# A state space layer on one core: table bursts moved to even steps, half of dt x B beside them, layer norm stretched, the mask's rows written later

## The chip, the core and the metric

The kernel runs on one core of a Trainium2 chip. A core has a matrix engine (TensorE, "PE" in the profile), three engines for elementwise work (VectorE "DVE", ScalarE "ACT", GpSimd "POOL"), and a queue engine (SyncE, "SP") from which this kernel issues all its transfers. The engines run side by side; each works through its own instructions in order and waits on semaphores where it needs another's result. The metric is the device time of one execution in microseconds (us). Lower is better.

## The reference

Two layers act on x of shape (4, 384, 64, 64). Both are added to their input, and both first normalise it over 32 groups of channels.

The first layer is a state space model over the 4096 positions of each image. Cut to what matters here:

```python
xn = layernorm(groupnorm(x)) over the 384 channels
xb, z = in_proj(xn)                    # 2 x 768 channels
xc = silu(causal_conv4(xb) + conv_b)
dt_r, B, C = x_proj(xc)                # 24 + 16 + 16
dt = softplus(dt_w @ dt_r + dt_b)      # 768 channels
h[t] = exp(dt[t] * A) * h[t-1] + (dt[t] * xc[t]) * B[t]     # 16 states a channel
y[t] = sum over states of h[t] * C[t] + D * xc[t]
out = out_proj(y * silu(z))
```

The second layer is attention in a window of 7 x 7 around each pixel, 12 heads, with a bias `rel_bias` for each head and place in the window.

## The kernel before

**Chunks and steps.** The first layer takes the 4 images one after the other, each in 11 chunks of 372 or 376 positions (44 chunks). A chunk has `STEPS` = 24 steps: 6 blocks of 128 channels (d) times 4 groups of 4 states (g). One step, in the loop over s (lines 752 to 829), does for group s:

- ScalarE: four decays exp(dt * A) (`decay`, into 3 buffers in PSUM called da);
- VectorE: four scans along the positions (`scan`, one for each state), which leave h;
- GpSimd: the multiply of the group before, h(s-1) by C, in place, and one half of a dt x B product for a later group;
- TensorE: the sums of h(s-2) over the states, by transposing matmuls into one accumulator (`sums`).

**dt x B.** The input of a scan, "db", is dt * xc times B for four states. Groups of even number get theirs from VectorE, of odd number from GpSimd, each in two halves of two states (`drive`). VectorE reads dt * xc from PSUM (dtxps), GpSimd from a copy (dtx). VectorE makes the first half for group s+2 in step s and the second half in step s+1, each between its first and its second scan (line 773).

**The state.** The last column of each scan is copied away by ScalarE (line 778), since GpSimd then overwrites h. The copy for group s-1 is placed in step s, after two decays of group s. GpSimd's multiply waits for it.

**Work of other chunks.** All that prepares a chunk (load, group norm `gn`, layer norm `ln_mean`, `ln_by`, `ln_square`, `ln_var`, `ln_rstd`, then `in_proj`, `conv`, `x_proj`, `dt_mm`, loads of weights and of rows of B and C) and all that finishes it (`gate`, `out_proj`, `residual`, statistics of the output) is spread by hand over the steps of the chunks before and after. `put(o, kind, fn)` (lines 555 to 607) puts a function o steps after the chunk's first step into a list of that step; `run(s, kind)` carries it out at a fixed place of the step: one task of ScalarE between decay 2 and decay 3 (or the dtx copy there, in every third step of four), the others after the scans, then the burst, then TensorE's tasks, VectorE's, the statistics ("STAT"), and at the end SP's. The class `Written` keeps each engine's instructions in that order. Matmul results go to one of 3 PSUM banks (`bank`), handed out in turn.

**Bursts.** The decays need the table of exp; silu and softplus need other tables. So for each chunk there are three bursts on ScalarE (`silu` of xc, `softplus`, `silu` of z; lines 447 to 504): a table load, six activations, a table load back. They stand at steps 14, 19 and 3 of a chunk (offsets -10, -5 and 3). In `softplus`, two dt matmuls are made ahead, and each activation frees a bank for the next one.

**Statistics of an image.** While an image runs, the next image's x is loaded and its group statistics taken (`batch_stats`); `stats_steps` (lines 178 to 225) then spreads them over channels in five pieces, on TensorE, VectorE and ScalarE.

**The mask.** The attention needs its bias as a table in DRAM (bm) that is filled with a large negative number and then written in rows of seven by 96 transfers (lines 160 to 174), ahead of everything else of the first layer on SP's queue. The attention layer reads it at its start (line 1117).

Of the kernel before, what the change touches and what calls it, by code (L numbers as in the profile page):

```python
# [30 lines left out]
TM = max(SIZES)  # L31
TB = 3
STEPS = ND * NQ
TX = 512
NXT = L // TX
GROUPS = 32
# [46 lines left out]
def two_layers(  # L83
# [77 lines left out]
    with tc.tile_pool(name="fill", bufs=1) as fpool:  # L161
        fill = fpool.tile([QB, NH * NK], F32, name="fill")
        nc.gpsimd.memset(fill, MASKED)
        nc.sync.dma_start(bm, fill)
    with nc.allow_non_contiguous_dma(reason="rows of seven, once"):
        for qi in range(RB):
            for h in range(NH):
                dst = bass.AP(
                    bm.tensor,
                    bm.offset + qi * (CB * NH * NK + CW) + h * NK,  # L170
                    [[NH * NK + 1, CB], [CW, WS], [1, WS]],
                )
                src = rel_bias[h].unsqueeze(0).broadcast_to([CB, WS, WS])
                nc.sync.dma_start(dst, src)

    x1s = [dram.tile([C, L], F32, tag="x1", name=f"x1_{b}", bufs=NB) for b in range(NB)]

# [49 lines left out]
    def state_space_layer(eng):  # L227
# [5 lines left out]
        with ExitStack() as es:  # L233
# [49 lines left out]
            def tile_of(shape, tag, bufs, home=sb):  # L283

                if tag not in free:
                    free[tag] = [
                        home.tile(shape, F32, name=f"{tag}{k}") for k in range(bufs)
                    ]
                    for t in free[tag]:
                        kind_of[id(t)] = tag  # L290
                return free[tag].pop(0)
# [17 lines left out]
            def at(step, fn, *args):  # L309
                todo.setdefault(step, []).append((fn, args))  # L310
# [174 lines left out]
            def dt_mm(X, d):  # L485
                T = chunks[X][3]
                made[X]["dtp", d] = ps = bank()
                te.matmul(
                    ps[:, :T], w_dt[:, d * P : (d + 1) * P], made[X]["xd"][:DTR, :T],
                    start=True, stop=True,  # L490
                )
                if d == ND - 1:
                    done(made[X].pop("xd"))

            def softplus(X):
                T = chunks[X][3]
                for d in range(ND):
                    t = made[X]["dt", d] = tile_of([P, TM], "dt", 7)
                    ps = made[X].pop(("dtp", d))
                    se.activation(t[:, :T], ps[:, :T], AF.Softplus, bias=dtb[:, d : d + 1])  # L500
                    done(ps)
                    if d + 2 < ND:
                        dt_mm(X, d + 2)
                exp_tables()


# [49 lines left out]
            for X, (b, i, t0, T) in enumerate(chunks):  # L556
                S = STEPS * X

                def put(o, kind, fn, *args, S=S, X=X):
                    at((S + o, kind), fn, X, *args)  # L560

                put(-44, SP, load_x)
                for j in range(NJ):
                    put(-40 + j, ACT, gn, j)
                put(-36, PE, ln_mean)
                put(-34, DVE, ln_by, "mu", ALU.subtract)
                put(-33, ACT, ln_square, 0)
                put(-33, ACT, ln_square, 1)
                put(-32, PE, ln_var, 0)
                put(-32, PE, ln_var, 1)  # L570
                put(-32, ACT, ln_square, 2)
                put(-31, PE, ln_var, 2)
                put(-30, ACT, ln_rstd)
                put(-29, DVE, ln_by, "rs", ALU.mult)
                put(-29, ACT, halo)
                for d, o in enumerate((-26, -25, -24, -22, -20, -18)):
                    put(o - 3, SP, load_w, d)
                    put(o, PE, in_proj, d)
                    put(o + 1, ACT, in_bias, d)
                for d, o in enumerate((-23, -21, -19, -17, -15, -13)):  # L580
                    put(o, PE, conv, d)
                    put(o + 1, ACT, conv_bias, d)
                put(-10, BURST, silu, "xc")
                put(-9, PE, x_proj, 0)
                put(-8, PE, x_proj, 1)
                put(-7, ACT, x_rows)
                for k, o in enumerate((-11, -10, -9, -7, -4, -4)):
                    put(o - 3, SP, load_w, ND + k)
                    put(o, PE, in_proj, ND + k)
                    put(o + 1, ACT, in_bias, ND + k)  # L590
                for d in range(2):
                    put(-6, PE, dt_mm, d)
                put(-5, BURST, softplus)
                for o, which, g in (
                    (-4, "B", 0), (-3, "B", 1), (-2, "B", 2), (-2, "C", 0),
                    (-1, "B", 3), (-1, "C", 1), (0, "C", 2), (1, "C", 3),
                ):
                    put(o, SP, load_bc, which, g)
                put(3, BURST, silu, "z")
                for d in range(ND):  # L600
                    put(4 * d + 8, DVE, gate, d)
                for o, m, half in ((29, 0, 0), (30, 0, 1), (32, 1, 0), (33, 1, 1), (36, 2, 0), (36, 2, 1)):
                    put(o, PE, out_proj, m, half)
                for m, load_at, o, so in ((0, 28, 31, 38), (1, 31, 34, 38), (2, 35, 38, 43)):
                    put(load_at, SP, load_res, m)
                    put(o, DVE, residual, m)
                    put(so, DVE, out_stats, m)

            def batch_stats(b):
                S = STEPS * NCHUNK * b  # L610
                pieces = [(j, k) for k in range(NCHUNK) for j in range(NJ)]
                for n, (j, k) in enumerate(pieces):
                    o = S - STEPS * NCHUNK + STEPS * (n // 4) + (3, 3, 19, 19)[n % 4]
                    cell = []

                    def begin(j=j, k=k, cell=cell):
                        cell.append(x_stats(b, j, k))

                    def use(cell=cell):
                        cell.pop()()  # L620

                    at((o - 3, SP), begin)
                    at((o, DVE), use)
                cell = []

                def start():
                    cell.append(x_norm(b))

                at((S - 51, DVE), start)
                for k in range(5):  # L630
                    at((S - 50 + k, "STAT"), lambda: next(cell[0]))

            for b in range(1, NB):
                batch_stats(b)
            for b in range(NB):
                cell = []

                def begin(b=b, cell=cell):
                    cell.append(
                        stats_steps((te, ve, se.activation, done), mv1[b], gm1[b], bank, f"b{b}")  # L640
                    )

                S = STEPS * (NCHUNK * (b + 1) - 1)
                at((S + 44, "STAT"), begin)
                for k in range(5):
                    at((S + 44 + k, "STAT"), lambda cell=cell: next(cell[0]))


            cell = []
# [15 lines left out]
            def run(step, kind, only=None):  # L665
                tasks = todo.get((step, kind), [])
                part = tasks if only is None else tasks[:only]
                if only is not None:
                    todo[step, kind] = tasks[only:]
                else:  # L670
                    todo.pop((step, kind), None)
                for fn, args in part:
                    fn(*args)
# [4 lines left out]
            def drive(engine, r, half):  # L678
                X, d, T = block(r)
                g = groups[r][2]  # L680
                if half == 0:
                    drives[r] = tile_of([P, NG, TM], "db", 3)
                src = dtxps if engine is ve else dtx[X, d]
                sl = slice(2 * half, 2 * half + 2)
                engine.tensor_tensor(
                    drives[r][:, sl, :T], src[:, :T].unsqueeze(1).broadcast_to([P, 2, T]),
                    made[X]["B", g][:, sl, :T], ALU.mult,
                )
                if half == 1 and d == ND - 1:
                    done(made[X].pop(("B", g)))  # L690
                if half == 1 and g == NQ - 1:
                    done(dtx.pop((X, d)))
# [56 lines left out]
                    )  # L749
                done(yt)  # L750

            for s in range(-44, N + 28):
                r = s if 0 <= s < N else None
                g = s % NQ

# [13 lines left out]

                half = s % 2  # L770
                q = s + 2 - half
                if 0 <= q < N:
                    drive(ve, q, half)
                if 0 <= s - 1 < N:
                    X, d, T = block(s - 1)
# [38 lines left out]
                if g == 1 and (k := at_block(-3)):  # L814
                    X, d, T = k
                    se.copy(dtxps[:, :T], made[X]["dt", d][:, :T])
                run(s, DVE)
                run(s, "STAT")
                q = s + 1 + half
# [356 lines left out]
```

## Time and profile before

| what | value |
|---|---|
| median of 3 runs (lowest to highest) | 7939.66 us (7924.37 to 7944.17) |
| the profiled execution, its own time | 7920.43 us |
| its span in the profile | 7918.7 us |
| busy: PE, DVE, ACT, POOL | 6700.7, 6161.5, 5183.3, 6065.7 us |
| start until GpSimd's first dt x B (prologue) | 222.2 us |
| from there to the end of the last multiply by C | 5628 us |
| the attention layer after it | 2068 us |

Lines in the profile name an engine, an operation and the tiles as out<-in. Nearly all instructions have the line L66, that of the helper that keeps the order, so they are told apart by tiles: "h<-da,state,db" is a scan, "da" a decay, "db" a half of dt x B, "h<-h,BC" the multiply by C, "state<-h" the copy of the state, "dt<-mm" a softplus, "xc<-xc" and "sz<-sz" the silus, "mm<-mm" the two activations of `ln_rstd`. What stands after a vertical bar or in square brackets is idle time of the engine just before, and what ended it. SPq is the time in which SP issues a transfer.

### The profile page before, as it was taken

Reading aid. Unit: us, or ns where it says so; the run is one execution under the profiler, and the core shown is the slowest. Engines: PE = TensorE matmul, PEld = TensorE weight load, DVE = VectorE, ACT = ScalarE, POOL = GpSimd, SP = SyncE. Lnnn points to the kernel's source line nnn. Section 1 sums busy time; section 2 is a strip of 40 time slices with the busy share of each in tenths; the row PEclk is TensorE's granted clock in tenths of the full one; section 3 lists DMA queues with packets and bytes.
Section 4 is the critical chain, followed back from the end, with each engine's and each line's share of the span. In section 5 each row is a group of like instructions: output and inputs, shape, how many; then the busy total and the mean of one; then the engine's idle time right before and its main releaser. Section 6 shows DMA issues by size and latency. Waiting matters only on the chain.

```text
span 7918.7 us, 133479 instructions
## 1 busy us (share of the span) xinstructions
PE 6700.7 (85%) x46968; PEld 4369.9 (55%) x46968; DVE 6161.5 (78%) x10561; ACT 5183.3 (65%) x12246; POOL 6065.7 (77%) x3015
## 2 busy tenths in 40 slices
PE   3888888888888888888888888888879899899998
PEld 2555555555555555555555655555545455455555
DVE  1799999999999999999998999999955444444444
ACT  1777777777777767777777777777735455455555
POOL 0899999999999999999998999999964333333333
PEclk9899999999999999999999999999889999999999
DMA  2323323132323222232322222222223222222332
GB/s 83 97 75 97 94 76 100 62 101 69 99 74 96 84 76 89 82 95 73 104 67 92 64 92 68 90 84 77 86 59 96 91 90 91 90 91 90 96 95 80
DMA packets 467012, 677.10 MB, mean 86 GB/s; under 512 B 48317, under 2 KB 424397, under 8 KB 466149
## 3 DMA queue, kind: packets, MB, share of 16 engines
q1 hardware_dynamic: 466340, 668.56, 27.3%
q8 instruction: 371, 6.08, 0.3%
q14 instruction: 301, 2.46, 0.1%
HBM read 582.92 MB, written 85.65 MB: 84 GB/s over the span
## 4 chain that ended last, share of the span: by engine, by line
DVE 29%; PE 28%; ACT 16%; issue 10%; POOL 9%; DMA 5%; SPq 3%; DVEq 0%; POOLq 0%; ACTq 0%
DVE h L66 20%; PE mm L66 17%; POOL h L66 6%; DVE db L66 5%; ACT da L66 5%; ACT L66 4%; PE pt L66 3%; POOL db L66 3%; PE yps L66 3%; DMA o<-x 3%; SPq L66 2%; PE lg L66 2%; PE ov L66 2%; ACT sz L66 2%; ACT xc L66 2%
## 5 line engine op out<-in xcount | busy, mean ns | idle before, releaser
L66 DVE TENSOR_TENSOR_SCAN h<-da,state,db 128x372 f32<-128x372 f32 (+1 forms) x3840 | 3581.6, 983 | 384.5 <-ACT da L66 288.3
L66 POOL TENSOR_TENSOR h<-h,BC 128x1488 f32<-128x1488 f32 (+1 forms) x1056 | 3541.4, 3354 | 291.9 <-ACT state L66 291.5
L66 ACT ACTIVATE da<-dt,nega 128x372 f32<-128x372 f32 (+1 forms) x4224 | 2378.9, 572 | 614.4 <-DVE h L66 597.0
L66 PE MATMUL yps<-ident,h 128*124 128x128 f32 (+1 forms) x12672 | 1764.6, 294 | 555.1 <-POOL h L66 536.3
L66 PEld LDWEIGHTS yps<-ident,h 128*124 128x124 f32 (+1 forms) x12672 | 1558.9, 150 | 903.1 <-POOL h L66 808.3
L66 POOL TENSOR_TENSOR db<-dtx,BC 128x744 f32<-128x744 f32 (+1 forms) x1056 | 1882.9, 1783 | 59.2 <-DMA BC<-bcrows 47.6
L66 POOL TENSOR_TENSOR sg<-sg,rs 128x784 f32<-128x784 f32 x384 | 573.2, 1493 | 1025.9 <-DVE rs L66 895.4
L66 ACT ACTIVATE sg<-sg,mx 128x196 f32<-128x196 f32 x1536 | 684.8, 447 | 779.0 <-DVE mx L66 777.9
L66 PE MATMUL mm<-xn,w_in 128*128 128x372 f32 (+3 forms) x3168 | 1148.9, 503 | 9.7 <-ACT sz L66 5.8
L66 DVE TENSOR_TENSOR db<-dtxps,BC 128x744 f32<-128x744 f32 (+1 forms) x1056 | 966.6, 915 | 1.2 <-DMA BC<-bcrows 0.6
L66 PEld LDWEIGHTS mm<-xn,w_in 128*128 128x128 f32 x3168 | 610.2, 205 | 361.6 <-issue 60.8
L66 PE MATMUL mm<-xb,dcv 128*128 128x372 f32 (+1 forms) x2112 | 719.8, 484 | 0.0
L66 DVE CUSTOM_DVE_ANT_0 sg<-lg,bias 128x196 f32<-128x196 f32 x1536 | 462.6, 357 | 298.1 <-PE lg L66 297.8
L66 PE MATMUL mm<-xp,w_qkv 128*128 128x512 f32 x1092 | 539.1, 632 | 116.7 <-DVE o L66 116.2
L66 PE MATMUL mm<-yg,w_out 128*128 128x372 f32 (+1 forms) x1584 | 540.9, 483 | 0.0
L66 PEld LDWEIGHTS mm<-xb,dcv 128*128 128x128 f32 x2112 | 397.3, 195 | 225.2 <-issue 13.3
L66 PE MATMUL pt<-ident,sg 128*98 128x128 f32 x3072 | 420.2, 279 | 4.1 <-ACT pT L66 2.3
L66 PEld LDWEIGHTS pt<-ident,sg 128*98 128x98 f32 x3072 | 319.3, 128 | 122.3 <-issue 109.4
L66 PEld LDWEIGHTS mm<-xp,w_qkv 128*128 128x128 f32 x1092 | 205.5, 202 | 323.4 <-issue 191.9
L66 PE MATMUL yps<-ident,xD 128*124 128x128 f32 (+1 forms) x792 | 152.7, 306 | 263.6 <-ACT yt L66 261.7
L66 DVE TENSOR_TENSOR_SCAN h<-da,db 128x372 f32<-128x372 f32 x384 | 334.1, 916 | 49.7 <-ACT da L66 37.2
L66 PEld LDWEIGHTS mm<-yg,w_out 128*128 128x128 f32 x1584 | 290.1, 194 | 145.2 <-issue 7.0
(111 smaller groups left out, 7149.4 us busy)
## 6 DMA issues: line engine op xcount, KB each, us to landing
BC<-bcrows SPq DMA_DIRECT2D x320, 744.0 KB
w_in<-wdr SPq DMA_DIRECT2D x528, 192.0 KB
vw<-vdr SPq DMA_DIRECT2D x512, 147.0 KB
xs<-in_x_dram SPq DMA_DIRECT2D x240, 186.0 KB
vdr<-v SPq DMA_DIRECT2D x280, 96.0 KB
xp<-x SPq DMA_DIRECT2D x32, 768.0 KB
o<-x SPq DMA_DIRECT2D x96, 256.0 KB
out_dram<-o SPq DMA_DIRECT2D x96, 256.0 KB
```

What stands on the lines that cost most here:

```text
L66: ins = made(*args, **kw)
```

## The change

- The mask's 96 transfers become tasks of SP, one at the end of each of the steps 24 to 119.
- The bursts stand at steps 14, 18 and 4 of a chunk (`BURSTS`). In these steps VectorE's second half of dt x B for group s+2 is made after the burst's scans, in the same step, and no longer in the step after.
- `softplus` has three dt matmuls made ahead, and its tiles are 8 instead of 7.
- The layer norm of a chunk begins 7 steps earlier and takes longer: load at -51 instead of -44, mean at -46 instead of -36, squares one a step from -40, `ln_rstd` at -35 instead of -30, the last multiply at -34 instead of -29.
- VectorE's work on whole tiles (the two operations of layer norm, input and output statistics) moves to the steps of the bursts.
- `x_proj`, `x_rows`, the second half of `in_proj` and the dt matmuls move by a step or two.
- The statistics of the next image begin 16 steps earlier, and their five pieces are spread over steps -66, -64, -63, -62 and -56 instead of five in a row.

```diff
+BURSTS = (4, 14, 18)
...
-    with nc.allow_non_contiguous_dma(reason="rows of seven, once"):
-        for qi in range(RB):
-            for h in range(NH):
...
-                nc.sync.dma_start(dst, src)
+    def mask_row(dq, qi, h):
+
+        dst = bass.AP(
+            bm.tensor,
+            bm.offset + qi * (CB * NH * NK + CW) + h * NK,
+            [[NH * NK + 1, CB], [CW, WS], [1, WS]],
+        )
+        with nc.allow_non_contiguous_dma(reason="rows of seven, once"):
+            dq.dma_start(dst, rel_bias[h].unsqueeze(0).broadcast_to([CB, WS, WS]))
...
-                    t = made[X]["dt", d] = tile_of([P, TM], "dt", 7)
+                    t = made[X]["dt", d] = tile_of([P, TM], "dt", 8)
...
-                    if d + 2 < ND:
-                        dt_mm(X, d + 2)
+                    if d + 3 < ND:
+                        dt_mm(X, d + 3)
...
-                put(-44, SP, load_x)
+                put(-51, SP, load_x)
                 for j in range(NJ):
-                    put(-40 + j, ACT, gn, j)
-                put(-36, PE, ln_mean)
-                put(-34, DVE, ln_by, "mu", ALU.subtract)
-                put(-33, ACT, ln_square, 0)
-                put(-33, ACT, ln_square, 1)
-                put(-32, PE, ln_var, 0)
-                put(-32, PE, ln_var, 1)
-                put(-32, ACT, ln_square, 2)
-                put(-31, PE, ln_var, 2)
-                put(-30, ACT, ln_rstd)
-                put(-29, DVE, ln_by, "rs", ALU.mult)
-                put(-29, ACT, halo)
+                    put(-50 + j, ACT, gn, j)
+                put(-46, PE, ln_mean)
+                put(-44, DVE, ln_by, "mu", ALU.subtract)
+                for j in range(NJ):
+                    put(-40 + j, ACT, ln_square, j)
+                    put(-37 + j // 2, PE, ln_var, j)
+                put(-35, ACT, ln_rstd)
+                put(-34, DVE, ln_by, "rs", ALU.mult)
+                put(-33, ACT, halo)
...
-                put(-8, PE, x_proj, 1)
-                put(-7, ACT, x_rows)
-                for k, o in enumerate((-11, -10, -9, -7, -4, -4)):
+                put(-9, PE, x_proj, 1)
+                put(-8, ACT, x_rows)
+                for k, o in enumerate((-11, -10, -8, -5, -4, -3)):
...
-                for d in range(2):
-                    put(-6, PE, dt_mm, d)
-                put(-5, BURST, softplus)
+                for d in range(3):
+                    put(-7, PE, dt_mm, d)
+                put(-6, BURST, softplus)
...
-                put(3, BURST, silu, "z")
+                put(4, BURST, silu, "z")
...
-                for m, load_at, o, so in ((0, 28, 31, 38), (1, 31, 34, 38), (2, 35, 38, 43)):
+                for m, load_at, o, so in ((0, 28, 31, 38), (1, 31, 34, 42), (2, 35, 38, 42)):
...
-                    o = S - STEPS * NCHUNK + STEPS * (n // 4) + (3, 3, 19, 19)[n % 4]
+                    o = S - STEPS * NCHUNK + STEPS * (n // 4) + (4, 4, 18, 18)[n % 4]
...
-                at((S - 51, DVE), start)
-                for k in range(5):
-                    at((S - 50 + k, "STAT"), lambda: next(cell[0]))
+                at((S - 67, DVE), start)
+                for k in (6, 8, 9, 10, 16):
+                    at((S - 72 + k, "STAT"), lambda: next(cell[0]))
...
+            for qi in range(RB):
+                for h in range(NH):
+                    at((24 + qi * NH + h, SP), mask_row, dq, qi, h)
...
-            for s in range(-44, N + 28):
+            for s in range(-51, N + 28):
...
-                if 0 <= q < N:
+                if 0 <= q < N and (half == 0 or (s - 1) % STEPS not in BURSTS):
                     drive(ve, q, half)
...
+                if s % STEPS in BURSTS and 0 <= s + 2 < N:
+                    drive(ve, s + 2, 1)
                 run(s, DVE)
```

More of the change, by code (lines that the diff above doesn't have):

```diff
@@ L164, in two_layers @@
         nc.sync.dma_start(bm, fill)
-    with nc.allow_non_contiguous_dma(reason="rows of seven, once"):
-        for qi in range(RB):
-            for h in range(NH):
[L168 to L174, printed above, removed]
+    def mask_row(dq, qi, h):
[6 more added lines that the diff above has]
+            dq.dma_start(dst, rel_bias[h].unsqueeze(0).broadcast_to([CB, WS, WS]))
     x1s = [dram.tile([C, L], F32, tag="x1", name=f"x1_{b}", bufs=NB) for b in range(NB)]
```

## The prediction

> **What bounds the kernel now.** First the page, for the busiest engine of the first layer:
>
> ```profile
> L66 POOL TENSOR_TENSOR h<-h,BC 128x1488 f32<-128x1488 f32 (+1 forms) x1056 | 3541.4, 3354 | 291.9 <-ACT state L66 291.5
> ...
> L66 POOL TENSOR_TENSOR db<-dtx,BC 128x744 f32<-128x744 f32 (+1 forms) x1056 | 1882.9, 1783 | 59.2 <-DMA BC<-bcrows 47.6
> ```
>
> One pair per step: overlapped, POOL needs 5.03 us a step (the spacing of its h rows where nothing waits), 24 steps make 120.7 us a chunk. Then the busy times of that stretch:
>
> ```profile
> 222.00:5850.00 5628.00, 4716.80 (x22620) 3250.89 (x22618) 5172.13 (x6306) 4124.93 (x8505) 5320.72 (x2130) 0.93 0.27 83
> ```
>
> POOL (fifth figure) works 5321 of 5628 us, VectorE (third) 5172. So the layer can lose at most 307 us of POOL idling. The view of waits names nearly all of it:
>
> ```profile
> POOL h L66 <- ACT state L66: 291.5, 126, 6.7
> ```
>
> The timeline of one softplus burst (the sixth of 44, in step 19 of the chunk before its own) shows the place:
>
> ```profile
> 831.41 1.28 ACT L66 ACT_TABLE_LOAD   x1
> ...
> 840.78 0.18 ACT L66 COPY state<-h 128x4 f32<-128x4 f32 x1
> 841.04 3.34 POOL L66 TENSOR_TENSOR h<-h,BC 128x1488 f32<-128x1488 f32 x1 [4.28 <-ACT state L66]
> ```
>
> POOL's multiply of group r waits for the state copy of r, which stands on ScalarE behind the burst and two decays of r+1. It had been scanned at 834.27. Call **lead** of r the time from the end of its last scan to its POOL multiply. POOL idles at burst b by (state copy − scan end) − lead. Summed over POOL's rows by place in the chunk: 42 us at step 3, 49 at 14, 171 at 19; an ordinary chunk (29 of 44) idles 5.99 us.
>
> How the lead grows: a VectorE step takes 4.37 us, or 4.82 with one more 0.45 us operation (dt multiply, gate, residual), so the lead gains 0.66 or 0.21 a step; after every burst it is 1.2.
>
> Last, the start of the kernel, in the timeline:
>
> ```profile
> 13.75 15.49 PE L66 MATMUL pb<-lnb,w_in 128*128 128x1 f32 x72 [13.75 <-DMA w_in<-in_in_wT_dram]
> 15.04 65.51 SPq L174 DMA_DIRECT2D bm<-in_rel_bias_dram  x96
> ...
> 97.60 8.14 SPq L66 DMA_DIRECT2D wdr<-w_in  x12
> ```
>
> 96 mask transfers hold SP's queue; the weights behind them come at 80.6, and ScalarE, VectorE and all that follows stand still.
>
> **What the Trainium skill says.** "ScalarE: Activation LUTs", What ACT_TABLE_LOAD costs: 1283 ns a load, and some 1380 ns of drain at a switch. The trace agrees on 1.28; the next activation follows 1.30 after the load's start, so no further drain is added here. "TensorE: Matmul & The Clock Gate", Part 1: PE falls to half rate after about one idle window of 3.4 us. The trace agrees: within softplus, one dt matmul pair takes 0.62 us in some chunks and 1.24 in others. The same page, array detail: PE's queue can only pull weight loads ahead; matmuls keep their order, which the PE rows below show too. "SBUF — State Buffer", two separate sides: VectorE with two SBUF inputs and GpSimd lock each other out for a whole instruction. At the batch statistics a 128x3 operation takes 3.25 us beside POOL, against 0.16 in the prologue.
>
> **The change, part by part.**
>
> *Mask.* The loads then wait for nothing but the fill's landing (15.0). The bias matmul ends at 29.24 and becomes the next late thing; from its copy to the first wdr issue it is 2.98 us (94.62 to 97.60), so that issue falls at 32.2, 65.4 earlier. Three gn (0.69 us each) of the third chunk and their load now stand ahead of step 0: −3. Net 62. The 96 issues return in steps 24 to 119, 0.68 us of SP each; SP issues some 31 transfers of about 0.4 us per 126 us, and what is queued behind (weights, B and C rows) is wanted two or more steps, 10 us, later. Cost 0; uncovered, 96 x 0.68 = 65 us.
>
> *Half of dt x B into the burst.* 0.83 us of VectorE leaves the step after each burst. That step is 3.65 instead of 4.48 us after its first decay, so the lead after a burst is 0.6 + 5.03 − 3.65 = 1.98 instead of 1.2.
>
> *Softplus, one matmul deeper.* From the first softplus to the end of the sixth takes 3.7 to 6.0 + 0.57 us now (offsets of the rows in all 44 chunks, mean about 5.4). With three banks filled ahead, three pairs remain: 3.4 us at full PE rate, 5.3 at half rate; I take 4.0. No xD copy (0.5) follows, since step 18 is not a third step of four.
>
> *Bursts at 4, 14, 18.* State copy after scan end: at 14 as now, 4.62 + 0.6 = 5.2. At 18 the burst starts 1.7 before the scan end (dt x B, dtx copy, last decay come first): −1.7 + 1.3 + 4.0 + 1.3 + 0.65 + 0.6 = 6.2. At 4, 3.6 (burst 5.14, no xD).
>
> *Layer norm stretched.* ln_rstd now is ScalarE's task in step 13, between decays 2 and 3, and waits for the last ln_var, which stands on PE in step 12 behind two halves of the output projection. The rows that show that queue:
>
> ```profile
> 790.48 2.67 PE L66 MATMUL mm<-xb,dcv 128*128 128x372 f32 x8
> ...
> 795.20 3.92 PE L66 MATMUL mm<-yg,w_out 128*128 128x372 f32 x12
> ...
> 798.09 0.57 ACT L66 ACTIVATE da<-dt,nega 128x372 f32<-128x372 f32 x1 [0.61 <-DVE h L66]
> ...
> 798.95 2.04 PE L66 MATMUL mm<-xn,ones_c 128*128 128x372 f32 x6
> ```
>
> Two ln_var (0.63 each, a third of the mean's 1.88) follow the convolution: the sums of step 12 start at 794.25 instead of 793.83, the last ln_var ends at 800.05, and rstd (0.96) and decay 3 end at 801.6. But decay 3 of step 13 went at 798.09. PE follows POOL (its sums wait for POOL), so this is fixed against POOL's start at 805.50: the scan ends at 802.7 and **the lead at 13 is held to 2.8**, where it would be 4.6. In the same way conv_bias(4), behind the mean on PE, holds the lead at 4 to 4.8.
>
> *The rest.* VectorE's whole-tile work (layer norm 1.25, output and input statistics 0.45 each, gate) now lies in the bursts: 3.4 us with the half of dt x B at 4, 3.0 at 14, 2.6 at 18, all inside the scan-free times of 3.0 to 4.8, 4.6 and 5.6; what does not fit would be paid one for one. x_proj, x_rows and in_proj of z move by a step or two: same counts, and PE's steps 13 to 17 hold under 4 us of work each, so PE's idle time hides them; uncovered, one in_proj is 1.9 us.
>
> The ledger of leads: 1.98 at 19, 5.4 at 4 (held to 4.8: idle 0.54), 1.98 at 5, 4.6 at 13 held to 2.8, 3.0 at 14 (idle 5.2 − 3.0 = 2.2), 1.98 at 15, plus 0.66, 0.21, 0.21 = 3.06 at 18 (idle 6.2 − 3.06 = 3.14). Sum 5.88 against 5.99: over the 29 ordinary chunks 3 us. What the bursts gain, the rstd wait takes.
>
> *Next chunk's load.* load_x at −51 needs the buffer whose last reader runs on PE in that very step, 3.4 us before POOL's multiply of step 21. 0.4 us to the issue, then about 4.3 us: the transfer of 558 KB ended 6.3 us after issue with 1.1 MB queued ahead, at a peak 390 KB/us. gn in step 22 waits some 0.7 us; hidden by the spare lead at 4.
>
> *Batch statistics.* The three boundaries now idle 11.5 us over an ordinary chunk (16.4, 19.7, 16.4). Spread out, the locked operations still cost 4.9, and 1.4 and 0.6 at the next bursts: 6.9. Gain 4.6 x 3 = 14; the second layer's statistics, with a burst at 4 instead of 3: 3 x 1.5 = 4.5. Bound: 0 to 30.
>
> Sum: 62 + 3 + 14 + 4.5 = about 84. Profiled execution 7920.4 (span 7918.7) gives 7836; the median of the runs lies 19 above the profiled time, so 7939.7 − 84 = **7856**.
>
> **Rivals.**
> 1. *The lead survives at 13* (ln_var runs earlier than I count, or PE keeps full rate). Then the lead at 14 is 4.8, idle 0.45, and with 3.4 us of softplus 2.5 at 18: 3.5 a chunk, 2.4 less, 40 x 2.4 = 96 more: 7760. For it: PE is only 84% busy; against it: step 12's own rows.
> 2. *Slower: ScalarE waits for xn in step 22.* Queue order there is fixed, so every us of gn's wait is taken from the lead. Up to 2.4 us the way to step 4 absorbs it (6.0 without wait, 3.6 needed); beyond, each costs 44 us. It takes the 84 us and a measurable loss from a wait of about 5 us, a landing 8.6 us after issue; a wait of 6: 44 x 3.6 − 84 = +74, 8015. Against it: 6.3 us was the longest landing I found, with more ahead.
> 3. *Softplus always at half PE rate*: 1.3 us more a chunk, 57 us: 7913.
> 4. *Mask issues cost as much in the loop as before it*: 62 lost, 7918.
>
> **How the numbers follow.** Forecast 0.52 (7810 to 7895), rival 1 0.24, rival 2 0.07, rivals 3 and 4 0.17. Range 7745 to 7935: it leaves out most of rival 2 and the best of rival 1. About 0.3% (24 us) is what a measurement can tell here. Faster: 0.52 + 0.24 + most of 3 and 4 (0.09) = 0.85; within 0.3%: 0.08; slower: 0.07.
>
> **What would show it.** wdr issued near 32 us and the first POOL multiply near 169 instead of 231. A new wait of ScalarE's rstd on PE of 1.5 to 2 us, 44 times; POOL idle of about 0.5, 2.2 and 3.1 us at steps 4, 14 and 18, and the chunk still near 126.5 us. The softplus activations 0.62 or 1.24 apart for the last three only. Wrong if the chunk falls to 124 us or below, or rises over 128.

## The result and the profile after

| | before | after |
|---|---|---|
| median of 4 runs (lowest to highest) | 7934.56 us (7924.37 to 7944.17) | 7829.76 us (7823.9 to 7842.14) |
| span of the profiled execution | 7918.7 us | 7822.2 us |
| start until GpSimd's first multiply by C | 231.0 us | 163.9 us |
| from there to the end of the last one | 5619.4 us | 5589.4 us |
| attention layer | 2068.3 us | 2068.9 us |

The ratio of the times is 0.987, with a 95% interval of 0.9852 to 0.9888. The three stretches of the span give -67.1, -30.0 and +0.6: together the 96.5 us by which the span is shorter.

The lines that answer to those of before follow. (The helper's line is L67 now.) First the page's group of GpSimd's multiplies:

```profile
L67 POOL TENSOR_TENSOR h<-h,BC 128x1488 f32<-128x1488 f32 (+1 forms) x1056 | 3540.4, 3353 | 263.1 <-ACT state L67 247.0
```

One multiply is as long as before (3353 ns); only the idle time ahead of them fell, from 291.9 to 263.1 us. The start of the kernel, from the timeline of SP's queue and of TensorE (start, length, operation):

```profile
15.70 0.37 SPq L146 DMA_DIRECT2D w_xp<-in_xp_wT_dram  x1
...
32.92 8.12 SPq L67 DMA_DIRECT2D wdr<-w_in  x12
...
14.41 15.49 PE L67 MATMUL pb<-lnb,w_in 128*128 128x1 f32 x72 [14.41 <-DMA w_in<-in_in_wT_dram]
```

The weights come at 15.7 instead of 80.6, the bias matmul ends at 29.90 and is what the folding of the weights now waits for, and the first wdr issue falls at 32.92 instead of 97.60.

Then the burst that the prediction showed, one step earlier in the chunk, from ScalarE's and GpSimd's timelines:

```profile
759.29 1.28 ACT L67 ACT_TABLE_LOAD   x1
760.59 2.74 ACT L67 ACTIVATE dt<-mm,dtb 128x372 f32<-128x372 f32 x5
763.81 0.57 ACT L67 ACTIVATE dt<-mm,dtb 128x372 f32<-128x372 f32 x1 [0.48 <-PE mm L67]
...
766.71 0.18 ACT L67 COPY state<-h 128x4 f32<-128x4 f32 x1
...
766.96 3.33 POOL L67 TENSOR_TENSOR h<-h,BC 128x1488 f32<-128x1488 f32 x1 [2.93 <-ACT state L67]
```

The group had been scanned at 760.96; its state is copied at 766.89. GpSimd idles 2.93 us here, where it idled 4.28.

Last, steps 11 to 13 of that chunk, from TensorE's and ScalarE's timelines:

```profile
724.16 1.41 PE L67 MATMUL mm<-sq,ones_c 128*128 128x372 f32 x4
725.41 1.47 PE L67 MATMUL yps<-ident,h 128*124 128x128 f32 x12
726.72 3.92 PE L67 MATMUL mm<-yg,w_out 128*128 128x372 f32 x12
730.48 0.79 PE L67 MATMUL mm<-sq,ones_c 128*128 128x372 f32 x2
...
731.30 0.55 ACT L67 ACTIVATE mm<-mm,eps 128x372 f32<-128x372 f32 x1 [3.20 <-PE mm L67]
```

The third variance matmul stands behind the output projection, and rstd, on ScalarE between two decays, waits 3.2 us for it. Two waits of the whole run belong to this place (total, times, longest):

```profile
ACT mm L67 <- PE mm L67: 145.0, 44, 4.2
...
DVE yg L67 <- PE mm L67: 37.1, 40, 5.6
```

The first was predicted. The second, VectorE's gate, was not; it turns out to matter below.

GpSimd's idle time by place, averaged over the 26 chunks in which no image begins or ends in either kernel (worked out from its rows, as for before): 0.16, 2.68 and 2.84 us at steps 4, 14 and 18, in all 5.7, against 6.0. At 14 it is 2.1 us in 17 of them and 3.7 or 3.8 in nine.

What parts the two kinds is TensorE's clock. The trace records the clock that TensorE was granted: at any time it is either full or half (PEclk in a view by stretches, 1.00 or 0.50). In all 17 chunks with 2.1 us it was full in the 11 us ahead of the third variance matmul; in all nine others it was half in a part of them. Two lines of TensorE's timeline show it, the sums of step 11 in the chunk above and in the eighth chunk, which has 3.7:

```profile
719.97 1.53 PE L67 MATMUL yps<-ident,h 128*124 128x128 f32 x12 [2.51 <-POOL h L67]
...
1097.46 2.82 PE L67 MATMUL yps<-ident,h 128*124 128x128 f32 x12 [2.53 <-POOL h L67]
```

The matmuls are the same, and the idle time before them nearly so. From the first multiply by C to the end of the last, the record holds 806 us at half clock before and 471 after.

The next image's statistics fall in the tenth chunk of an image before and in the ninth after. In these two chunks of three images GpSimd idles 71.1 us in all before and 54.8 after.

### The profile page after: what moved, and what is told of

Same layout as the page of the kernel before. It is cut to its first block, busy times and chain, and to the rows that moved or that the text cites. A ratio compares the mean times of both kernels' runs of the same rounds, so it can differ in the third digit from the quotient of the medians.

```text
span 7822.2 us, 133481 instructions
## 1 busy us (share of the span) xinstructions
PE 6547.3 (84%) x46968; PEld 4271.8 (55%) x46968; DVE 6160.6 (79%) x10561; ACT 5158.4 (66%) x12246; POOL 6065.6 (78%) x3015
## 5 line engine op out<-in xcount | busy, mean ns | idle before, releaser
L67 DVE TENSOR_TENSOR_SCAN h<-da,state,db 128x372 f32<-128x372 f32 (+1 forms) x3840 | 3559.7, 979 | 342.1 <-issue 202.1
L67 POOL TENSOR_TENSOR h<-h,BC 128x1488 f32<-128x1488 f32 (+1 forms) x1056 | 3540.4, 3353 | 263.1 <-ACT state L67 247.0
L67 ACT ACTIVATE da<-dt,nega 128x372 f32<-128x372 f32 (+1 forms) x4224 | 2375.6, 571 | 488.4 <-DVE h L67 464.7
L67 PE MATMUL yps<-ident,h 128*124 128x128 f32 (+1 forms) x12672 | 1711.6, 289 | 755.7 <-POOL h L67 739.8
L67 PEld LDWEIGHTS yps<-ident,h 128*124 128x124 f32 (+1 forms) x12672 | 1487.6, 146 | 1166.6 <-POOL h L67 1060.5
L67 POOL TENSOR_TENSOR db<-dtx,BC 128x744 f32<-128x744 f32 (+1 forms) x1056 | 1885.9, 1786 | 56.1 <-DMA BC<-bcrows 40.8
L67 POOL TENSOR_TENSOR sg<-sg,rs 128x784 f32<-128x784 f32 x384 | 573.2, 1493 | 1029.4 <-DVE rs L67 879.1
L67 ACT ACTIVATE sg<-sg,mx 128x196 f32<-128x196 f32 x1536 | 684.8, 447 | 780.9 <-DVE mx L67 779.8
L67 PE MATMUL mm<-xn,w_in 128*128 128x372 f32 (+3 forms) x3168 | 1123.8, 492 | 43.9 <-ACT sz L67 37.5
L67 DVE TENSOR_TENSOR db<-dtxps,BC 128x744 f32<-128x744 f32 (+1 forms) x1056 | 963.0, 912 | 3.3 <-DMA BC<-bcrows 2.7
L67 PEld LDWEIGHTS mm<-xn,w_in 128*128 128x128 f32 x3168 | 586.4, 198 | 351.7 <-ACT sz L67 47.3
L67 PE MATMUL mm<-xb,dcv 128*128 128x372 f32 (+1 forms) x2112 | 719.2, 484 | 3.2 <-DVE xs L67 2.6
L67 DVE CUSTOM_DVE_ANT_0 sg<-lg,bias 128x196 f32<-128x196 f32 x1536 | 462.4, 357 | 295.1 <-PE lg L67 294.5
L67 PE MATMUL mm<-xp,w_qkv 128*128 128x512 f32 x1092 | 536.7, 630 | 121.9 <-DVE o L67 121.7
L67 PE MATMUL mm<-yg,w_out 128*128 128x372 f32 (+1 forms) x1584 | 534.5, 479 | 0.0
L67 PEld LDWEIGHTS mm<-xb,dcv 128*128 128x128 f32 x2112 | 397.3, 195 | 228.0 <-issue 12.1
L67 PE MATMUL pt<-ident,sg 128*98 128x128 f32 x3072 | 419.6, 279 | 4.7 <-ACT pT L67 2.7
L67 PEld LDWEIGHTS pt<-ident,sg 128*98 128x98 f32 x3072 | 318.3, 128 | 123.0 <-issue 107.7
L67 PEld LDWEIGHTS mm<-xp,w_qkv 128*128 128x128 f32 x1092 | 204.0, 200 | 325.7 <-issue 189.1
L67 DVE SCALAR_TENSOR_TENSOR o<-mm,pjb,o 128x512 f32<-128x512 f32 x96 | 72.1, 751 | 376.8 <-DMA o<-x 290.1
L67 DVE TENSOR_TENSOR_SCAN h<-da,db 128x372 f32<-128x372 f32 x384 | 332.6, 914 | 45.6 <-ACT da L67 25.2
L67 PEld LDWEIGHTS mm<-yg,w_out 128*128 128x128 f32 x1584 | 286.9, 192 | 142.4 <-issue 2.7
```

What stands on the lines that cost most here:

```text
L67: ins = made(*args, **kw)
```

## The experiments

Times compare as ratios to the kernel before, run on the same chip in the same session. The theory at this point was that of the prediction: the lead that the bursts gain is lost at step 13 to rstd's wait.

**The mask alone.** The kernel before, and only the mask moved.

```diff
-                nc.sync.dma_start(dst, src)
+                    at((24 + qi * NH + h, SP), mask_row, dq, qi, h)
```

> The kernel before, with the 96 mask transfers in steps 24 to 119 and nothing else of the change. Theory (the mask is the whole gain of the start and costs nothing in the loop): 65 us less than before, about 7869 us, first weight store near 33 us, first multiply by C near 165 us, and the stretch of the first layer unchanged at 5619 us from the first multiply to the last one's end. Rival 4 (the 96 issues cost as much in the loop): no change, 7934 us, with the stretch 60 us longer.

Measured: 7862.51 us against 7926.91, ratio 0.9921 (0.9906 to 0.9936). The first multiply starts at 166.3 us instead of 231.0: 64.7 earlier, and 64.4 us is what the time fell by. The stretch from the first multiply to the end of the last is 5626.7 us, 7.3 longer than before; the four times of this kernel differ by nearly twice as much (7856.34 to 7870.01). So the 96 issues cost little or nothing where they now lie; a cost of a few us cannot be told from this.

**Half of dt x B back in the step after the burst.**

```diff
-                if 0 <= q < N and (half == 0 or (s - 1) % STEPS not in BURSTS):
+                if 0 <= q < N:
...
-                if s % STEPS in BURSTS and 0 <= s + 2 < N:
-                    drive(ve, s + 2, 1)
```

> The kernel after, with VectorE's second half of dt x B back between the scans of the step after the burst. Theory (0.83 us of lead after each burst, of which the one at 18 alone is used, since the leads at 4 and 13 are held by TensorE): idle at 18 rises from 2.8 to 3.7 us, at 14 and 4 little changes: 0.9 x 40, some 35 us more than after, 7865 us. Rival (all three bursts gain 0.83 us): 100 us more, 7930 us. Rival (the half is hidden anyway): no change.

Measured: 7947.28 us, ratio 1.0027 (1.0016 to 1.0038): 0.0157 above after, some 125 us, and slower than before although the mask's 64 us are still in it. The ledger reads like this: leads after a burst are 1.15 us instead of 1.98, as the prediction had it; the idle at 14 is 3.7 instead of 2.7, at 18 4.9 instead of 2.8. Of the 2.1 us at 18, 0.8 is the lead; most of the rest is softplus, whose sixth activation starts 4.19 us after the first on average, instead of 3.24. So only 0.8 of the 3.1 us is the price that the expectation had counted. Most of the rest came with TensorE's clock: it was half for 792 us of the first layer instead of 471, and ahead of the third variance matmul it was half in part in 25 of the 26 chunks instead of nine. The view by stretches gives its mean over the first layer as the third number from the end, for the kernel after and then for this one:

```profile
163.90:5753.33 5589.43, 4563.45 (x22600) 3152.24 (x22600) 5165.24 (x6299) 4092.69 (x8490) 5315.81 (x2128) 0.96 0.26 83
...
164.28:5871.04 5706.76, 4691.05 (x22600) 3261.71 (x22600) 5162.12 (x6299) 4111.23 (x8490) 5315.20 (x2128) 0.93 0.25 81
```

This half of dt x B is worth more than all other edits of the loop together, and those others, without it, cost time: 7947 is 84 us over what the mask alone gives. The rival was nearer, and still too low.

**Two dt matmuls ahead instead of three.**

```diff
-                    if d + 3 < ND:
-                        dt_mm(X, d + 3)
+                    if d + 2 < ND:
+                        dt_mm(X, d + 2)
...
-                for d in range(3):
+                for d in range(2):
```

> The kernel after, with two dt matmuls ahead of softplus instead of three. Theory (the softplus burst lengthens by one matmul pair, and GpSimd's idle at 18 with it, one for one): the sixth softplus begins 4.4 us after the first on the mean instead of 3.2, idle at 18 rises from 2.8 to 4.0 us: 1.2 x 40, some 48 us more than after, 7878 us. Rival (the burst's length is covered by the lead): no change.

Measured: 7830.91 us, ratio 0.9883 (0.9868 to 0.9898), which overlaps the interval of after. The sixth softplus starts 3.25 us after the first, as with three ahead. The rival's number came, but not for its reason: the edit did not take the third pair of matmuls (one dt matmul is a pair of instructions) back behind the first softplus. TensorE's timeline of a burst before (its first softplus starts at 832.71) and of one in this run (at 892.0), four pairs each:

```profile
833.33 4.03 PE L66 MATMUL mm<-xd,w_dt 24*128 24x372 f32 x8 [1.73 <-ACT dt L66]
...
891.53 3.28 PE L67 MATMUL mm<-xd,w_dt 24*128 24x372 f32 x8
```

Before, the third pair waits for the first softplus to free a bank and starts 0.62 us or more after that softplus begins, in 43 of 44 bursts. In this run it starts ahead of the first softplus in 40 of 44, and within 0.3 us of its start in the others. By the order in which the kernels hand out their three banks, the reason is layer norm: before, its variance held a bank until VectorE's last multiply, behind the burst of step 19; now that multiply stands in step 14, and the third bank is free. So what puts the third pair ahead is the free bank, with `d + 3` or with `d + 2`. Its worth shows in the bursts themselves: at full clock the sixth softplus starts 3.72 us after the first before and 2.80 after, at half clock 5.98 and 4.75. The rest of the gain is the clock: bursts near the longer of these two times were 11 of 44 before and are 3 now.

**rstd's wait taken away.** All three variance matmuls in step 11.

```diff
-                    put(-37 + j // 2, PE, ln_var, j)
+                    put(-37, PE, ln_var, j)
```

> The kernel after, with the last ln_var in step 11 beside the other two, ahead of the output projection of step 12. Theory (the wait of ln_rstd behind that projection holds the lead at 13 to 2.8 us and takes what the bursts gain): ScalarE's wait before ln_rstd falls from 3.3 us to nothing, the lead at 14 rises from 3.0 to about 4.7, GpSimd's idle at 14 falls from 2.7 us to under 0.8 a chunk, at 18 it stays at 2.8: about 80 us less than after, 7750 us. Rival (TensorE is late as a whole, and the next task that waits for it, conv_bias in step 12 or in_bias in step 14, takes the place): under 20 us less, 7810 to 7830 us.

Measured: 7822.97 us, ratio 0.987 (0.9855 to 0.9885): no change. The wait itself is gone, and yet GpSimd idles 2.9 us at 14. The view of waits names the reason:

```profile
DVE yg L67 <- PE mm L67: 74.3, 42, 7.0
...
ACT mm L67 <- PE mm L67: 4.2, 2, 2.9
```

and the timelines of VectorE and TensorE show the place:

```profile
729.43 0.55 DVE L67 TENSOR_TENSOR yg<-mm,sz 128x372 f32<-128x372 f32 x1 [1.69 <-PE mm L67]
...
727.29 1.47 PE L67 MATMUL yps<-ident,h 128*124 128x128 f32 x12
728.60 2.67 PE L67 MATMUL mm<-yg,w_out 128*128 128x372 f32 x8
```

The gate of block 1, in step 12, writes yg. There are seven yg tiles, six are in use, the seventh went to the gate of step 8: the next comes free when `out_proj` of the chunk before has read it, and its last part runs on TensorE in step 12 too. With the variance matmuls ahead of it this part starts later, and VectorE, with the scans of step 13 queued behind the gate, stands. The new theory: two waits for the same late TensorE lie side by side, and removing one only leaves the other.

**Eight yg tiles.**

```diff
-                yg = made[X]["yg", d] = tile_of([P, TM], "yg", 7)
+                yg = made[X]["yg", d] = tile_of([P, TM], "yg", 8)
```

> The kernel after, with eight yg buffers in place of seven, so that the gate of block 1 at step 12 no longer needs the buffer that the second half of out_proj, on TensorE in the same step, still reads. Theory (two waits on TensorE's step 12 hold the lead at step 13, rstd's and this gate's; in the chunks with 3.7 us of idle at step 14 the gate's ends last, in the others rstd's): the idle at 14 falls from a mean of 2.7 to 2.1 us, the others stay: 7823 - 26 = about 7800 us. Rival (rstd's wait alone sets it): idle at 14 stays at 2.7, 7830 us.

Measured: 7838.07 us, ratio 0.9885 (0.9871 to 0.99): no gain. The gate's wait is down from 40 times to 2, but the idle at 14 stays at 2.9. So in the kernel after, rstd's wait is the last to end in all chunks, also in those with 3.8 us. What makes those longer is TensorE's clock, as the two lines of step 11 above show: with the sums at 2.82 us instead of 1.53, everything behind them comes 1.3 later.

**Both waits taken away.** Eight yg tiles and the variance matmuls in step 11.

```diff
-                    put(-37 + j // 2, PE, ln_var, j)
+                    put(-37, PE, ln_var, j)
...
-                yg = made[X]["yg", d] = tile_of([P, TM], "yg", 7)
+                yg = made[X]["yg", d] = tile_of([P, TM], "yg", 8)
```

> Eight yg buffers and, besides, the three variance matmuls of layer norm all in step 11 instead of 11, 11 and 12. Theory (with the variance matmuls early, rstd's wait is gone and the gate's wait took its place; with both gone the lead at step 13 is the natural 4.6 us): VectorE's stall of 2.2 us in steps 12 and 13 goes, idle of GpSimd at 14 about 0.6 instead of 2.9 us, 44 x 2.2 = 97 us less than 7823: about 7735 us. Rival (a third task behind TensorE's late step 12 takes the place again): idle at 14 stays over 2 us, 7800 to 7830 us.

Measured: 7795.86 us, ratio 0.9833 (0.9818 to 0.9848), 0.0037 below after. Either edit alone gained nothing, both together some 30 us: the waits do stand in for each other. The idle at 14 fell from 2.7 to 1.0 us (0.6 was expected). But at 18 it rose from 2.8 to 3.8: nearly half of the expected 97 us went there. From GpSimd's timeline, step 14 and 18 of the fifth chunk:

```profile
736.99 3.34 POOL L67 TENSOR_TENSOR h<-h,BC 128x1488 f32<-128x1488 f32 x1 [0.41 <-ACT state L67]
...
761.57 3.34 POOL L67 TENSOR_TENSOR h<-h,BC 128x1488 f32<-128x1488 f32 x1 [4.46 <-ACT state L67]
```

The lead at 18 is unchanged (it starts anew at each burst); softplus is longer: its sixth activation starts 4.10 us after the first on average, and 15 of 44 bursts take over 4.5. In the burst shown it starts 4.74 us after, with the last three pairs 1.25 apart. From just before the first softplus to the sixth, TensorE's granted clock is 0.68 on average over the 44 bursts, against 0.86 in the kernel after.

**The state's copy inside the burst.** The copy of a burst step's own group goes behind the third activation instead of behind the second table load and two decays.

```diff
                     se.activation(v, v, AF.Silu)
+                    if d == 2:
+                        keep_state(now[0])
```

(and the same in `softplus`; `keep_state` holds the copy that stood in the loop, which now skips groups that have been copied.)

> The kernel after, with the copy of the state of a burst step's group placed after the third of the burst's six activations instead of behind the burst. Theory A (GpSimd's idle at 14 and 18 is the wait for this copy and nothing else): both fall by 2.0 to 2.2 us, 44 x 4 = 176 us less, 7650 us. Theory B (VectorE's chain of scans, stalled by the whole burst, is nearly as long as GpSimd's, so that what GpSimd gains at one group it waits at a later one; the most to be had is VectorE's own wait for GpSimd at step 23, 1.1 us a chunk): 0 to 47 us less, 7785 to 7830 us.

Measured: 7773.75 us, ratio 0.9803 (0.9788 to 0.9817), 0.0067 or some 53 us below after. The copy costs no further table load, as the timeline shows:

```profile
753.19 1.49 ACT L67 ACTIVATE dt<-mm,dtb 128x372 f32<-128x372 f32 x3
754.56 0.20 ACT L67 COPY state<-h 128x4 f32<-128x4 f32 x1
755.45 0.57 ACT L67 ACTIVATE dt<-mm,dtb 128x372 f32<-128x372 f32 x1 [0.68 <-PE mm L67]
```

Both kernels have 265 loads. GpSimd no longer idles at 14 and 18. It idles one group later, 1.1 us at 15 and 3.4 at 19, because the scans of that group wait for the burst's end all the same. Theory A falls, and B is right, its 47 us a little too low. VectorE's idle time at step 23, 1.06 us a chunk before the edit, is 0.03: VectorE's chain of scans, with what the bursts stall it, is now as long as GpSimd's work.

**All three.**

```diff
+                    put(-37, PE, ln_var, j)
...
+                yg = made[X]["yg", d] = tile_of([P, TM], "yg", 8)
...
+                        keep_state(now[0])
```

> Eight yg buffers, the variance matmuls early and the state's copy inside the burst, all three. Theory B: the first two take VectorE's stall of 2.2 us in steps 12 and 13 away (7735 us), the third adds only what VectorE still waits for GpSimd, up to 1 us a chunk: 7690 to 7735 us. Theory A: the third adds 2.0 to 2.2 us at step 18 and 0.6 at 14 on top: 7735 - 120 = about 7615 us.

Measured: 7726.92 us, ratio 0.9742 (0.9722 to 0.9762), 0.0128 or 100 us below after. The pair alone gained some 30 us and the copy alone 53; together it is 100, and over the pair the copy gained 69, more than the 45 that B allowed: here B's bound fails, though the time lies in its range, since the pair had been expected to gain more. Why the bound fails is not shown. What is left is the idle at 19, 3.7 us, behind softplus, which takes over 4.5 us to its sixth start in 32 of 44 chunks. TensorE's timeline of such a burst:

```profile
743.67 2.14 PE L67 MATMUL mm<-xd,w_dt 24*128 24x372 f32 x6
748.28 0.90 PE L67 MATMUL yps<-ident,xD 128*124 128x128 f32 x3 [2.46 <-ACT yt L67]
748.97 2.76 PE L67 MATMUL yps<-ident,h 128*124 128x128 f32 x12
752.63 4.08 PE L67 MATMUL mm<-xd,w_dt 24*128 24x372 f32 x6 [0.90 <-ACT dt L67]
```

The same six instructions take 2.14 us and, behind a stretch with 2.5 us of idling, 4.08. That suggested keeping TensorE busy.

**Matmuls of no use ahead of softplus**, on the kernel with both waits gone, and on the one with all three edits.

```diff
+            def warm(X, n):
+                for k in range(n):
+                    te.matmul(yps[:, TB * P : 512], ident, ident, start=True, stop=True)
...
+                put(-8, PE, warm, 4)
+                put(-7, PE, warm, 8)
```

> Eight yg buffers and early variance matmuls, as in the run of 7796 us, plus twelve matmuls of 128x128 with no use (into columns of yps that nothing reads), four in step 16 and eight in step 17, where TensorE idles before softplus. Theory (freeing the lead at 13 gained 1.9 us at step 14, but TensorE then ran softplus's matmuls at half rate in nearly every chunk, six activations in 3.7 to 4.75 us instead of 2.8 to 3.4, and gave 1 us back at 18): with TensorE kept busy the sixth softplus activation starts 2.8 us after the first, the idle at 18 falls from 3.8 to about 2.5 us, 44 x 1.3 = 57 us less: about 7740 us. Rival (the extra matmuls hold up the sums, or the rate does not depend on this idle time): 7790 to 7830 us.

> The run of 7727 us (eight yg buffers, early variance matmuls, the state's copy inside the burst) plus the same twelve matmuls of no use in steps 16 and 17. Theory: softplus there took 4.75 us in nearly every chunk; at 2.8 us the idle at 19 falls from 3.7 to about 1.8 us, 44 x 1.9 = 84 us less: about 7645 us. Rival (the scan chain has no such slack, or the rate does not depend on this idle time): 7700 to 7740 us.

In these two kernels the four matmuls of step 16 restart the sum over states that is under way in the same PSUM bank, so that part of y is lost; the instructions and their number are those intended. "PSUM — Partial Sum Buffer", rule 2 on accumulation, in the Trainium skill has the mechanism: a matmul with the start flag clears the written marks of the whole bank, whichever bytes of it are written.

Measured: 7794.3 us, ratio 0.9833 (0.9816 to 0.9849), on the first, no gain over 7795.86; and 7685.09 us, ratio 0.9694 (0.9678 to 0.971), on the second, some 40 us below the kernel without them. In both, softplus became shorter (mean start of the sixth 4.10 to 3.37, and 4.23 to 3.29 us). On the first kernel the rival's first half is right: ScalarE's copy of finished sums waits for the extra matmuls, and with it the burst (117.4 us in 85 waits, against 53.6 in 45 without the extra matmuls).

```profile
753.92 0.48 ACT L67 COPY yt<-yps 124x384 f32<-124x384 f32 x1 [1.50 <-PE yps L67]
```

On the second, the idle at 19 fell from 3.7 to 2.1 us; the expected 1.8 us in every chunk and 7645 were too good, since some bursts, most of them near an image's boundary, stay slow. The copy waits much less there, 54.1 us in 46 waits; why is not shown.

**The same matmuls where they damage nothing.** First into unread columns of dtxps, in the kernel with all three edits:

```diff
-                    te.matmul(yps[:, TB * P : 512], ident, ident, start=True, stop=True)
+                    te.matmul(dtxps[:, TB * P : 512], ident, ident, start=True, stop=True)
```

> The run of 7685 us with its twelve extra matmuls written into unread columns of dtxps, a PSUM bank in which no sum is being gathered, instead of yps. Theory (TensorE's rate alone is what they change): as before, idle at 19 about 2.1 us, 7685 us (7665 to 7705). Rival (written into a bank that ScalarE and VectorE use, they wait for those engines and hold up the sums behind them): 7720 us or more.

Measured: 7761.54 us, ratio 0.9789 (0.9773 to 0.9805), worse than without them. The rival is right:

```profile
ACT dtxps L67 <- PE dtxps L67: 154.0, 43, 5.5
```

ScalarE's copy into that bank, with the dt x B products behind it, waits for TensorE in nearly every chunk, though the columns are others. Then into yps again, but with the start flag only behind the last sum of a block:

```diff
-            def warm(X, n):
+            def warm(X, n, start):
...
-                    te.matmul(yps[:, TB * P : 512], ident, ident, start=True, stop=True)
+                    te.matmul(
+                        yps[:, TB * P : 512], ident, ident,
+                        start=start, stop=start, skip_group_check=True,
+                    )
...
-                put(-8, PE, warm, 4)
-                put(-7, PE, warm, 8)
+                put(-8, PE, warm, 4, X == 0)
+                put(-7, PE, warm, 8, True)
```

> The run of 7685 us with the same twelve matmuls into yps, but those of step 16 without the start flag and only those of step 17, behind the last sum of a block, with it, so that no sum under way is restarted. Theory (the same work on TensorE at the same places, so the same rate in softplus): idle at 19 about 2.1 us, 7685 us (7665 to 7705). Rival (the gain of that run came of the damaged sums, not of the rate): 7727 us, as without the extra matmuls.

Measured: 7688.81 us, ratio 0.9699 (0.9683 to 0.9716). As the theory has it, so the gain came of TensorE's rate and not of the damaged sums. TensorE's timeline now:

```profile
744.40 2.05 PE L67 MATMUL yps<-ident 128*128 128x128 f32 x16
747.02 0.54 PE L67 MATMUL yps<-ident,xD 128*124 128x128 f32 x3 [0.57 <-ACT yt L67]
747.40 1.47 PE L67 MATMUL yps<-ident,h 128*124 128x128 f32 x12
750.60 2.14 PE L67 MATMUL mm<-xd,w_dt 24*128 24x372 f32 x6 [1.72 <-ACT dt L67]
```

The sums take 1.47 instead of 2.76 us and the dt matmuls of softplus 2.14 instead of 4.08. This is the granted clock, as the same view shows from the first to the sixth softplus, in the burst without the extra matmuls (0.50) and then in the one with them (1.00):

```profile
752.01:756.75 4.74, 4.12 (x7) 1.93 (x8) 2.98 (x6) 2.72 (x6) 4.74 (x3) 0.50 0.00 0
...
749.98:752.78 2.80, 2.18 (x7) 1.14 (x8) 2.80 (x6) 2.69 (x7) 2.80 (x3) 1.00 0.00 0
```

GpSimd idles 2.4 us an ordinary chunk, against 5.7 in the kernel after. This is the fastest version, 3.0% under the kernel before; about 140 us of that are beyond the change under study.

## Why the prediction was right, and where not

The forecast was 7856, the time is 7830. Of the 26 us between them, 12.5 are in the sum: 84 predicted, 96.5 found between the two spans. The other 13 lie in the step from a profiled execution to the median: the profile of before is 19 us under its median of then, that of after 6. Part of the agreement is luck: the loop's idle came out near the forecast because errors of 0.3 to 0.5 us at the three bursts cancel.

- *Mask: 62 predicted, 67 found,* and 64 when done alone. The wdr issue at 32.2 was right (32.92). The 3 us for the third chunk's norm did not show. Rival 4 falls.
- *Half of dt x B: right.* The lead after each burst is 1.98 to the hundredth, and 1.15 without the move. What the prediction did not see is how much of the change hangs on it, by way of TensorE's clock.
- *Softplus: right.* Its sixth activation ends 3.8 us after the first starts, 4.0 was taken, and the two bounds, 3.4 and 5.3, are 3.37 and 5.32. Three pairs remain, as the step read. But it is the bank that layer norm no longer holds that makes room for the third, not the third call ahead, as the run with two ahead shows. Where between the bounds the bursts lie hangs on TensorE's clock, for which the prediction had no working; 4.0 was chosen between them. Rival 3, always half rate, did not happen in this kernel, but came near with all three edits (32 of 44 bursts over 4.5 us).
- *The ledger of leads: right in the chunk shown, in part by chance.* Predicted idle 0.54, 2.2 and 3.14 us at 4, 14 and 18; found there 0.2, 2.1 and 2.9, on average 0.16, 2.7 and 2.8. The lead at 13 is 2.83 there, at 4 it is 4.79, as forecast (2.8, 4.8). But over the 26 chunks the lead at 13 is 2.8 in 17 and only 1.1 to 1.3 in nine, those with half clock. The 0.54 at 4 does not follow from the prediction's own numbers, since a lead of 4.8 covers the 3.6 that it gives for the state copy. The copy comes 4.7 us after the scan end in the chunk shown, 5.1 on average: the burst itself is held up as well. And the lead at 13 without the waits is 4.0 us, as the run without them shows, not 4.6.
- *"What the bursts gain, the rstd wait takes": right as to what ends last, incomplete as to what it hides.* The wait is there 44 times, 3.3 us on average and not 1.5 to 2, since ScalarE comes to it earlier than I counted. Rival 1, that the lead survives at 13 if the variance matmuls run earlier, fails for a reason that it did not have: the gate's buffer, behind the same matmuls. Rival 1's price was wrong too: with both waits away the idle at 14 falls to 1.0 and the gain is 30 us, not 96, because softplus then runs at half clock more often.
- *Batch statistics: 14 predicted, some 15 found* (71.1 to 54.8 in six chunks, less the 0.3 each that every ordinary chunk gained). Ordinary chunks gave 7 us over 26, predicted 3 over 29; the twelve others, with the second layer's statistics among them, 6, predicted 4.5. These shares are rough: with the mask alone moved, the ordinary chunks idle 9 us less than before and the twelve others 11 more.
- *Rival 2* (ScalarE waits for xn in step 22): the wait exists, 41.7 us over 37 times, 1.1 on average and 2.6 at most, far from the 5 at which it would have decided.

So the likeliest case was the one that came, with the mask as two thirds of it. What the chip added: the loop's small gain is a difference of large terms, +125 us for the half of dt x B and -84 for the rest, which the ledger had only as a net.

Left open: whether the bursts' new places or layer norm's stretching cost those 84 us; they were not undone separately. The idle times point to layer norm: with the half back, GpSimd idles 3.7 us at 14, where the burst has not moved, against 1.1 with the mask alone, and the lead at 13 is 1.2 instead of 3.9. That taking rstd's wait away changes nothing in the full kernel does not answer it.

## What to carry to other kernels

When a wait goes and the time stays, look at the same stretch for a second wait on the same late engine, here a buffer that its matmuls release, and remove both in one run; each alone reads as "no effect". Moving a release forward on the engine that waits helps only as far as the chain that feeds it has room: compare the two engines' idle time for each other first. And read the granted clock beside the length of a dependent chain of matmuls: here the same chain had two lengths, and an edit on VectorE changed how often each came.

## What the runs showed of the hardware

TensorE's two rates change on a fixed grid. In the kernel after, the record of the granted clock has 95 stretches at half clock in the first layer. Each begins and ends within 0.01 us of one grid of 3.4133 us, and each is a whole number of grid lengths, 66 of them one. "TensorE: Matmul & The Clock Gate", Part 1, in the Trainium skill states a free-running window of 3413 ns, and the trace agrees. The prediction had read the rate as a matter of idle length alone. It is one of place as well. Of the two idle stretches shown above, the one ahead of the fast sums (717.46 to 719.97) has a point of the grid inside it, at 718.42, with 0.96 us before it and 1.55 behind. The one ahead of the slow sums has 2.37 us in one window, which ends at 1097.30, and there the half clock begins. The 3.4 us of idle that the prediction took from that page was not needed here: 2.37 us within one window was enough.

What follows for a loop: the same idle stretch slows a burst in one chunk and not in the next, according to where the chunk falls on the grid. In the kernel with all three edits, the first softplus starts at most 0.8 us behind a grid point in ten bursts, and all ten take 2.8 us to the sixth; it starts 1.0 to 3.25 us behind one in 33, and 32 of these take 4.7 or 4.8; the last, 3.30 us behind, takes 2.8.

The loop can also settle on the grid. In the run with early variance matmuls, 20 of the 26 ordinary chunks took 126.3 or 126.4 us, and 37 windows are 126.29. There the first softplus of chunks two to eight starts 0.16, 0.41, 0.56, 0.67, 0.72, 0.75 and 0.76 us behind a grid point, and it comes to 0.73 to 0.80 in the other images too. What holds it there was not tested.
